# A graph attention layer on one core: messages behind the clip, two products set apart, and 186 instead of 169 column tiles

## The chip, the cores and the metric

The kernel runs on one core of a Trainium2 chip. The metric is device time in microseconds (us), the median of several runs. Engines are named as in the profile: PE (TensorE matmul), PEld (its weight load), DVE (VectorE), ACT (ScalarE), POOL (GpSimd) and SP (SyncE). "DVEq", "ACTq" and so on are the instruction sequencers of these engines, which read the engine's instructions in program order, wait for semaphores and load registers. L12 is line 12 of the kernel.

## What is computed

There are 6,250 nodes with 128 features and 206,250 directed edges, sorted by destination. Each edge has 128 features of its own. The layer is attention with eight heads of 16 features:

```python
Qh, Kh, Vh = (h @ WQ), (h @ WK), (h @ WV)          # per node, 8 heads x 16
Eh = edge_attr @ WE                                # per edge
score = einsum('ehd,ehd,ehd->eh', Kh[src], Qh[dst], Eh) / 4
score = exp(clip(score, -5, 5))
msg = Vh[src] * score[:, :, None]
wV = segment_sum(msg, dst); Z = segment_sum(score, dst)
x = layernorm(x + wV / (Z + 1e-6))
```

## The kernel before

**Tiles, batches, rounds.** The edges are cut into 1612 tiles of 128. Four tiles make a batch (smaller ones at the very end), 406 batches in all. The main loop has one round for each batch b, and different batches stand in it at different stages. From round 12 on the order of the instructions on each engine is the order in which the program writes them.

**Work of a round.** `stage_a(b)` is PE's: for each tile the Q rows of the destinations, by a product with a one-hot matrix (qps, L489), and the projected edge features (eps, L494). `stage_b(b-1)` is DVE's, in four steps between which the loop places other work: kq = K times Q (L500), kqe = kq times E (L503), the sum over each head (sc, L506), and the clip (L509). `weigh(b-1)` is ACT's: the exponential, written twice, into the PSUM tile exp_p (L515) and into the last columns of msg (L517). There is one buffer of exp_p. `messages(b-2)` is DVE's product of V and exp_p (msg, L548). `stage_c(b-2)` is PE's: it adds messages up by destination, with a one-hot matrix (agg, L570); ACT copies such sums to SBUF every fourth batch (L580). `stage_0` and `stage_0t` build the one-hot matrices on DVE for two batches at a time: onehot (L461) in even rounds, between kq and kqe, and onehotT (L477) in odd rounds, between kqe and the head sums.

**Fill steps.** `fill()` issues one small step of what is due beside the main work, if anything is: five DVE steps that split the Q rows of a block of 128 nodes (`q_rows`, L293 to L300), or a step of the normalisation of two blocks (`layernorm`, 22 DVE steps for two blocks, L773 to L793), which begins when ACT has copied its sums (fin, L541). A round has four such places.

**K and V of the sources.** They come into the tile kvrows in two ways. For most tiles POOL gathers 128 rows from a table in HBM (`gather`, L421; one indirect DMA a tile). For 169 tiles, every 11 batches five times, no rows are gathered: the 128 columns of x that belong to the sources are copied one by one out of the transposed x in SBUF (xz) into a tile xcol, PE projects them (`project_columns`, colkv, L403), and ACT places the result in kvrows (`place_columns`, L410). `column_tiles` chooses these tiles from COL0 and COLP.

**Columns.** `columns(b, v, most)` copies runs of COLN = 8 columns: for v = 0 on ACT, eight copies (L394), for v = 1 on DVE, four operations of two columns each (L390). Of the 16 runs of a tile the last six (COLV) are DVE's and ten ACT's. A column's address is read from a register. `addresses` issues the load of eight registers for a run (TENSOR_LOAD, L369), always one run ahead:

```python
at = ahead[v] or addresses(v)   # loaded with the run before
copied[v] += 1
ahead[v] = addresses(v)         # the load for the next run
...                             # then the copies of this run
```

So on each of the two engines the load for the next run stands directly ahead of the copies of this run. The count due grows evenly with b; DVE's 6 runs in 2.2 rounds are mostly three in a round, and the loop gives them three places, one run at each.

**DVE's order in a round** is: kq (b-1); onehot in even rounds; fill; kqe; onehotT in odd rounds; a run; fill; head sums; a run; messages (b-2); the rest of the runs due (one); fill; clip; fill. **ACT's** is: the copy of fin, if due; exp twice; placing; its runs of copies; the copy of agg, if due.

**Pace of the gathers.** The first gather of a batch waits for PE's qps of an earlier batch (`lag`: 12 batches before at first, falling to 3 by about batch 160).

Of the kernel before, what the change touches and what calls it, by code (L numbers as in the profile page):

```python
# [8 lines left out]
F32 = mybir.dt.float32  # L9
I32 = mybir.dt.int32  # L10
BF16 = mybir.dt.bfloat16
U8 = mybir.dt.uint8  # L12
# [4 lines left out]
P = 128  # L17
# [5 lines left out]
HW = 64  # L23
HALF = 16
DRIFT = 24
LEFT, RIGHT = 43, 128
XC = LEFT + N + RIGHT
MW = D + H
CH = 8
# [21 lines left out]
QLOOK = 3  # L51
QREG = 16
COL0 = 26
COLP = (11, 5)
COLN = 8
COLV = 6
COLL = 8
RING = 4096
SUMS = 8
XT_AT = RING + P  # L60
# [3 lines left out]
def cut_batches():  # L64
    out, t = [], 0
    while t < NT:
        k = B
        if t >= NT - TAIL:
            k = 2 if NT - t > 3 else 1
        out.append(range(t, t + k))  # L70
        t += k
    return out


def column_tiles():

    batches = cut_batches()
    at = (COL0 + k * COLP[0] // COLP[1] for k in range(len(batches)))
    return [batches[b][-1] for b in at if b < len(batches) and batches[b][-1] < NT - TAIL - 4 * B]
# [23 lines left out]
def edge_attention(ctx: ExitStack, tc: tile.TileContext, x, xT, srcT, srcC, dstT, dstB, dst0, bnd, lo, eaT,  # L103
                   wq, wkv, we, out, kv, qtab, qs, relD):
    nc = tc.nc
# [25 lines left out]
    nbat = len(batches)  # L131
    col_batches = [t // B for t in column_tiles()]
    col_half = (len(col_batches) + 1) // 2
    col_at = cp.tile([col_half, 2, P], I32, name="col_at")
# [4 lines left out]
    with ExitStack() as fast:  # L139
# [84 lines left out]
        def late_loads():  # L224
            if NT > C0:
                nc.sync.dma_start(src_sb[1], srcT[:, C0:])
                nc.sync.dma_start(dst_sb[:, C0:], dstT[:, C0:])
# [14 lines left out]
        wp = fast.enter_context(tc.tile_pool(name="work", bufs=3))  # L242
# [61 lines left out]
        def build_q(until, now):  # L304

            while qwork or (now and len(built) < until):
                if not qwork:
                    qwork.append(q_rows(len(built)))
                if next(qwork[0], None) is None:
                    qwork.pop()  # L310
                if not now:
                    break
# [23 lines left out]
        def load_chunk(c):  # L336
            if c in chunks or c * CH >= NT:
                return
            n = min(CH, NT - c * CH) * P
            tl = ep.tile([P, CH * P], F32, name="ea")  # L340
            nc.sync.dma_start(tl[:, :n], eaT[:, c * CH * P:c * CH * P + n])
            chunks[c] = tl
# [11 lines left out]
        col_tiles, xz_bytes = {}, xz.rearrange("p n z -> p (n z)").bitcast(U8)  # L354
# [1 line left out]

        copied, projected = [0, 0], []

        runs = P // COLN
        kinds = [range(runs - COLV), range(runs - COLV, runs)]  # L360
        ahead = [None, None]

        def addresses(v):

            k, j = divmod(copied[v], len(kinds[v]))
            if k >= len(col_batches):
                return None
            j = kinds[v][j] * COLN
            return nc.values_load_multi_w_load_instructions(  # L369
                col_at[k % col_half:k % col_half + 1, k // col_half, j:j + COLN],  # L370
                engines=((mybir.EngineType.Activation, mybir.EngineType.DVE)[v],),
                min_val=XT_AT + 8 * LEFT - 4, max_val=XT_AT + 8 * (LEFT + N - 1),
                skip_runtime_bounds_check_because="edges name nodes")[1]

        def columns(b, v, most=runs):

            mine = kinds[v]
            due = int((b - COL0 + COLL) * len(mine) * COLP[1] / COLP[0] + 1e-6)
            while most and copied[v] < min(due, len(col_batches) * len(mine)):
                k, j = divmod(copied[v], len(mine))  # L380
                at = ahead[v] or addresses(v)
                copied[v] += 1
                ahead[v] = addresses(v)
                most -= 1
                if k not in col_tiles:
                    col_tiles[k] = wp.tile([P, P], F32, name="xcol", bufs=5)
                to, j = col_tiles[k].bitcast(U8), mine[j] * COLN
                if v:
                    for c in range(0, COLN, 2):
                        nc.vector.tensor_tensor(to[:, 4 * (j + c):4 * (j + c) + 8], xz_bytes[:, ds(at[c] - XT_AT, 8)],  # L390
                                                xz_bytes[:, ds(at[c + 1] - XT_AT, 8)], op=ALU.bitwise_or)
                else:
                    for c in range(COLN):
                        nc.scalar.copy(to[:, 4 * (j + c):4 * (j + c) + 4], xz_bytes[:, ds(at[c] - XT_AT, 4)])  # L394

        def project_columns(b):

# [8 lines left out]
        def place_columns():  # L406

            while projected:
                g, pk = projected.pop()
                nc.scalar.copy(g[:, B - 1, :], pk)  # L410
# [135 lines left out]
        def messages(b):  # L546
            n, g, m = st8[b]
            nc.vector.tensor_tensor(  # L548
                m[:, :n, :D].rearrange("p b (h d) -> p b h d", h=H),
                g[:, :n, D:].rearrange("p b (h d) -> p b h d", h=H),  # L550
                exp_p[:, :n, :, None].to_broadcast([P, n, H, DH]), op=ALU.mult)
# [47 lines left out]
        build_q(q_built(QLOOK + 2), True)  # L599
        nc.sync.dma_start(col_at, srcC.rearrange("(h p) e -> p h e", h=2))  # L600
        nc.vector.tensor_scalar(col_at, col_at, 8, XT_AT + 8 * LEFT, op0=ALU.mult, op1=ALU.add)
        odd = col_at[:, :, (runs - COLV) * COLN:].rearrange("k h (c z) -> k h c z", z=2)[:, :, :, 1]
        nc.vector.tensor_scalar(odd, odd, 4, None, op0=ALU.subtract)
        load_rel(0)
        for j in range(QLOOK):
# [2 lines left out]
        def fill():  # L608

            if qwork:  # L610
                build_q(0, False)
            elif norms and next(norms[0], None) is None:
                norms.pop(0)

        held = []
        for b in range(nbat + 3):
            if b >= XB and not manual:
                manual.append(fast.enter_context(tc.manual_schedule()))
            held += [(b + SLAG, store) for store in stores]
            stores.clear()  # L620
            if held and (held[0][0] <= b or b >= nbat):
                held.pop(0)[1]()
            if b < nbat:
                load_chunk(batches[b][0] // CH + EB - 3)
                load_rel(batches[b][0] // RC + 1)
                load_q(batches[b][0] // WT + QLOOK)
                g = gathered.pop(b)
                if b == min(XB, nbat - 1):
                    late_loads()
                if b == min(XB + 8, nbat - 1):  # L630
                    relative(C0, NT)
                if b == 14:
                    from_window(1)
                if b == 0:
                    stage_0t(0)
                stage_a(b, g)
                if b + GLEAD < nbat and b + GLEAD not in gathered:
                    gathered[b + GLEAD] = gather(b + GLEAD)
            norms.extend(pending)
            pending.clear()  # L640
            for _ in range(len(ready) if b >= nbat - 2 else 1):
                if ready:
                    finish(ready.pop(0))
            steps = stage_b(b - 1) if 0 <= b - 1 < nbat else iter(())
            next(steps, None)
            if b < nbat:
                stage_0(b)
            fill()
            next(steps, None)
            if b + 1 < nbat:  # L650
                stage_0t(b + 1)
            if b < nbat:
                columns(b, 1, 1)
            fill()
            next(steps, None)
            if b < nbat:
                columns(b, 1, 1)
            if 0 <= b - 2 < nbat:
                messages(b - 2)
            if b < nbat:  # L660
                columns(b, 1)
            fill()
            next(steps, None)
            fill()
            if 0 <= b - 1 < nbat:
                weigh(b - 1)
            place_columns()
            if b < nbat:
                columns(b, 0)
            if 0 <= b - 2 < nbat:  # L670
                stage_c(b - 2)
            if b < nbat:
                project_columns(b + GLEAD)
                build_q(q_built(min(NJ - 1, batches[b][0] // WT + QLOOK + 2)), True)
                if not qwork and len(built) < q_built(
                        min(NJ - 1, batches[min(nbat - 1, b + 3)][0] // WT + QLOOK + 2)):
                    qwork.append(q_rows(len(built)))
                    next(qwork[0])
            if b == min(60, nbat):
                count_inside()  # L680
            if b == min(80, nbat + 1):
                inside = nc.values_load(cnt_i[0:1, 0:1], min_val=0, max_val=2 * EPAD,
                                        skip_runtime_bounds_check_because="two counts of EPAD edges")
# [159 lines left out]
```

## Time and profile before

| | us |
|---|---|
| median of 3 runs | 1866.14 (1864.48 to 1867.87) |
| the profiled execution: its time | 1863.48 |
| the profiled execution: its span | 1861.6 |
| busy: DVE | 1710.0 (92%) |
| busy: ACT | 1576.9 (85%) |
| busy: POOL | 1379.2 (74%) |
| busy: PE, weight loads | 1324.9 (71%), 1156.1 (62%) |
| granted clock of TensorE, mean | 0.927 |

The span is the time between the first and the last instruction on the profiled core. The page gives, for each group of instructions of one line and form, the count, the busy time, the mean duration in ns of one, and behind the second bar the time for which the engine had stood idle just before one of them, with what ended most of it ("issue": nothing that the profile shows). Durations on DVE overlap: an operation that doesn't need the result of the one before starts before that one has ended, so that the distance from start to start, read in the timeline, is what it costs. A register load is executed by the sequencer and does not count as busy.

### The profile page before, as it was taken

To read this page: it belongs to the slowest core of one execution; us is meant where nothing else is said; L and a number is where in the kernel's file an instruction comes from. 1 tells how busy PE (TensorE), PEld (TensorE's weight loads), DVE (VectorE), ACT (ScalarE), POOL (GpSimd) and SP (SyncE) were. 2 spreads that over 40 slices of the span, in tenths; PEclk is the share of its full clock that TensorE was granted. 3 is DMA by queue.
4 is the path that set the end of the run, shared out by engine and by line. 5 is a ranking of instruction groups with operands and counts; after the bars stand their busy time and mean duration, and the time that the engine had idled before them with its cause. 6 is when DMAs were issued, how large, how long until landed. Compare 5 with 4: busy or idle time off the path is not lost.

```text
span 1861.6 us, 49514 instructions
## 1 busy us (share of the span) xinstructions
PE 1324.9 (71%) x9388; PEld 1156.1 (62%) x9388; DVE 1710.0 (92%) x7312; ACT 1576.9 (85%) x14716; POOL 1379.2 (74%) x1450
## 2 busy tenths in 40 slices
PE   5877777677677767777767776776767676777775
PEld 4766666566566666666656665665656665666665
DVE  6579999999999999999999999999999999999986
ACT  3327999899999999999999999999989998999950
POOL 7777777767777777677777777777777777777774
PEclk8888998899999999899998899899999999999997
DMA  9767677667766776677677667767766676677652
GB/s 303 228 214 217 184 217 206 197 187 207 212 199 183 212 214 184 209 214 208 183 225 210 190 188 225 206 184 211 224 202 185 202 223 190 196 200 233 205 173 68
DMA packets 170093, 377.79 MB, mean 203 GB/s; under 512 B 58305, under 2 KB 84245, under 8 KB 169775
## 3 DMA queue, kind: packets, MB, share of 16 engines
q0 software_dynamic: 68480, 186.02, 34.7%
q1 hardware_dynamic: 100155, 187.47, 33.6%
q14 instruction: 241, 1.97, 0.3%
q8 instruction: 77, 1.26, 0.3%
q10 hardware_dynamic: 1140, 1.06, 0.2%
HBM read 359.61 MB, written 14.81 MB: 201 GB/s over the span
## 4 chain that ended last, share of the span: by engine, by line
DVE 38%; DMA 17%; ACT 16%; PE 9%; POOL 7%; issue 6%; DVEq 5%; ACTq 2%; SPq 0%; POOLq 0%
DMA kvrows<-kv,src 14%; ACT xcol L394 13%; DVE xcol L390 7%; POOL kvrows L421 7%; DVE kqe L503 6%; DVE kq L500 6%; DVE sc L506 6%; DVE msg L548 5%; DVEq L369 5%; PE agg L570 3%; DVE onehotT L477 2%; PE eps L494 2%; ACTq L369 2%; PE finps L529 1%; DVE sc L509 1%
## 5 line engine op out<-in xcount | busy, mean ns | idle before, releaser
L421 POOL DMA_INDIRECT kvrows<-kv,src x1395 | 1329.7, 953 | 445.1 <-issue 307.7
L394 ACT COPY xcol<-xz 128x4 uint8 x13520 | 1364.8, 190 | 55.0 <-issue 49.4
L570 PE MATMUL agg<-msg,onehot 128*128 128x136 f32 x3224 | 511.6, 305 | 283.7 <-DVE msg L548 216.6
L570 PEld LDWEIGHTS agg<-msg,onehot 128*128 128x128 f32 x3224 | 442.0, 206 | 335.9 <-issue 302.6
L494 PE MATMUL eps<-we_sb,ea 128*128 128x128 f32 x3224 | 494.3, 299 | 149.3 <-DVE kqe L503 110.8
L494 PEld LDWEIGHTS eps<-we_sb,ea 128*128 128x128 f32 x3224 | 423.7, 205 | 200.2 <-DVE kqe L503 149.8
L390 DVE TENSOR_TENSOR xcol<-xz 128x8 uint8 x4056 | 399.5, 157 | 2.8 <-issue 1.7
L500 DVE TENSOR_TENSOR kq<-kvrows,qps 128x512 f32<-128x512 f32 x406 | 273.4, 673 | 38.3 <-DMA kvrows<-kv,src 29.0
L503 DVE TENSOR_TENSOR kqe<-kq,eps 128x512 f32<-128x512 f32 x406 | 274.5, 676 | 19.7 <-PE eps L494 4.7
L548 DVE TENSOR_TENSOR msg<-kvrows,exp_p 128x512 f32<-128x512 f32 x406 | 272.9, 672 | 4.6 <-ACT exp_p L515 4.6
L506 DVE TENSOR_REDUCE sc<-kqe 128x32 f32<-128x512 f32 x406 | 271.0, 667 | 0.5
L489 PE MATMUL qps<-qw,onehotT 126*128 126x128 bf16 x1612 | 168.6, 230 | 39.0 <-DVE kq L500 32.6
L489 PEld LDWEIGHTS <-onehotT 126*128 126x128 bf16 x1612 | 134.3, 103 | 84.9 <-issue 58.4
L515 ACT ACTIVATE exp_p<-sc 128x32 f32<-128x32 f32 x406 | 79.3, 195 | 92.1 <-DVE sc L509 79.3
L461 DVE TENSOR_TENSOR onehot<-iota_p,dst_sb 128x512 f32<-128x512 f32 x200 | 135.9, 680 | 3.0 <-PE agg L570 3.0
L529 PE MATMUL finps<-sum,shift 128*128 128x136 f32 x640 | 94.8, 292 | 30.0 <-ACT sum L580 29.8
L403 PE MATMUL colkv<-wkv_sb,xcol 128*128 128x256 f32 x338 | 114.5, 424 | 0.0
L477 DVE TENSOR_SCALAR onehotT<-relb,node 126x1024 bf16<-126x1024 bf16 (+2 forms) x206 | 103.7, 504 | 9.7 <-DMA relb<-relD 9.7
L529 PEld LDWEIGHTS finps<-sum,shift 128*128 128x128 f32 x640 | 83.3, 197 | 37.4 <-ACT sum L580 37.3
L517 ACT ACTIVATE msg<-sc 128x32 f32<-128x32 f32 x406 | 87.1, 215 | 0.1
L509 DVE TENSOR_SCALAR sc<-sc 128x32 f32<-128x32 f32 x406 | 77.0, 190 | 0.3
L421 POOL DMA_INDIRECT kvrows<-x,src x48 | 48.6, 1012 | 16.5 <-issue 12.2
(76 smaller groups left out, 567.2 us busy)
## 6 DMA issues: line engine op xcount, KB each, us to landing
ea<-eaT SPq DMA_DIRECT2D x201, 512.0 KB
relb<-relD SPq DMA_DIRECT2D x100, 504.0 KB
kvrows<-kv,src POOLq DMA_INDIRECT x1395
qw<-qs SPq DMA_DIRECT2D x202, 31.5 KB
kv<-ea SPq DMA_DIRECT2D x12, 512.0 KB
qs<-qst SPq DMA_DIRECT2D x48, 96.0 KB
xb<-x SPq DMA_DIRECT2D x24, 128.0 KB
out<-h SPq DMA_DIRECT2D x24, 128.0 KB
```

Source lines behind the costliest of these rows:

```text
L390: nc.vector.tensor_tensor(to[:, 4 * (j + c):4 * (j + c) + 8], xz_bytes[:, ds(at[c] - XT_AT, 8)], xz_bytes[:, ds(at[c + 1] - XT_AT, 8)], op ...
L394: nc.scalar.copy(to[:, 4 * (j + c):4 * (j + c) + 4], xz_bytes[:, ds(at[c] - XT_AT, 4)])
L421: ins = nc.gpsimd.indirect_dma_start(out=g[:k, i, :f], out_offset=None, in_=rows, in_offset=bass.IndirectOffsetOnAxis(ap=src_col(t)[:k], a ...
L477: nc.vector.tensor_scalar(ohT[:, :w], rels[t0 // RC][:, e0:e0 + w], node[:QROWS], None, op0=ALU.is_equal)
L489: expanded[b] = nc.tensor.matmul(pq[:, i, :], ohT[:, i * P:i * P + P], loaded[t0 // WT], start=True, stop=True)
L494: nc.tensor.matmul(pe[:, i, :], ea[:, i * P:i * P + P], we_sb, start=True, stop=True)
L500: nc.vector.tensor_tensor(t0[:, :n], g[:, :n, :D], pq[:, :n], op=ALU.mult)
L503: nc.vector.tensor_tensor(t1[:, :n], t0[:, :n], pe[:, :n], op=ALU.mult)
L506: nc.vector.tensor_reduce(sc[:, :n], t1[:, :n].rearrange("p b (h d) -> p b h d", h=H), axis=AX.X, op=ALU.add)
L529: nc.tensor.matmul(ps, shift[:, P - s:2 * P - s], sums[k // 2][:, k % 2], start=first and i == 0, stop=stop and i == len(parts) - 1)
L548: nc.vector.tensor_tensor(m[:, :n, :D].rearrange("p b (h d) -> p b h d", h=H), g[:, :n, D:].rearrange("p b (h d) -> p b h d", h=H), exp_p[ ...
L570: nc.tensor.matmul(aggs[u][:, 0 if final else k % 2], oh[:, i, :], m[:, i, :], start=not final and t % (2 * G) == 0, stop=tail)
```

## The change

The diff does these things:

- COLP goes from (11, 5) to (2, 1): a column tile every two batches, 186 instead of 169. DVE's six runs a tile are then three in every round, and ACT's ten are five.
- The cut into runs is written in a new way (COL2 = 8, COLV = 48 columns); the runs are the same as before, eight columns each, ten of ACT's and six of DVE's.
- The order on DVE becomes: kq (b-1); in even rounds onehot, in odd rounds a fill and one run; kqe; in odd rounds onehotT, in even rounds one run; two fills; head sums; the rest of the runs due (two); fill; clip; messages (b-2). The next round's kq follows.
- The transposed x loses its margins (LEFT 43 and RIGHT 128 become 1 and 1), and xcol has six buffers instead of five.

```diff
-LEFT, RIGHT = 43, 128
+LEFT, RIGHT = 1, 1
...
-COLP = (11, 5)
+COLP = (2, 1)
 COLN = 8
-COLV = 6
+COL2 = 8
+COLV = 48
...
-                    col_tiles[k] = wp.tile([P, P], F32, name="xcol", bufs=5)
+                    col_tiles[k] = wp.tile([P, P], F32, name="xcol", bufs=6)
...
             if b < nbat:
                 stage_0(b)
-            fill()
+            if b % 2:
+                fill()
+            if b < nbat and b % 2:
+                columns(b, 1, 1)
             next(steps, None)
             if b + 1 < nbat:
                 stage_0t(b + 1)
-            if b < nbat:
+            if b < nbat and b % 2 == 0:
                 columns(b, 1, 1)
             fill()
+            fill()
             next(steps, None)
-            if b < nbat:
-                columns(b, 1, 1)
-            if 0 <= b - 2 < nbat:
-                messages(b - 2)
             if b < nbat:
                 columns(b, 1)
             fill()
             next(steps, None)
-            fill()
+            if 0 <= b - 2 < nbat:
+                messages(b - 2)
             if 0 <= b - 1 < nbat:
                 weigh(b - 1)
             place_columns()
```

`next(steps, None)` issues, in this order, kq (ahead of the lines shown), kqe, the head sums and the clip.

More of the change, by code (lines that the diff above doesn't have):

```diff
@@ L357, in edge_attention @@
         copied, projected = [0, 0], []
-        runs = P // COLN
-        kinds = [range(runs - COLV), range(runs - COLV, runs)]
+        mid = P - COLV
+        few, pairs2 = -(-mid // COLN), COLV // COL2
+        cut = [mid * i // few for i in range(few + 1)] + [mid + COL2 * (i + 1) for i in range(pairs2)]
+        pieces = list(zip(cut, cut[1:]))
+        kinds = [pieces[:few], pieces[few:]]
         ahead = [None, None]
@@ L367, in addresses @@
                 return None
-            j = kinds[v][j] * COLN
+            i, j = kinds[v][j]
             return nc.values_load_multi_w_load_instructions(
-                col_at[k % col_half:k % col_half + 1, k // col_half, j:j + COLN],
+                col_at[k % col_half:k % col_half + 1, k // col_half, i:j],
                 engines=((mybir.EngineType.Activation, mybir.EngineType.DVE)[v],),
@@ L373, in addresses, with columns @@
                 skip_runtime_bounds_check_because="edges name nodes")[1]
-        def columns(b, v, most=runs):
+        def columns(b, v, most=P):
             mine = kinds[v]
@@ L385, in columns @@
                 if k not in col_tiles:
-                    col_tiles[k] = wp.tile([P, P], F32, name="xcol", bufs=5)
-                to, j = col_tiles[k].bitcast(U8), mine[j] * COLN
+                    col_tiles[k] = wp.tile([P, P], F32, name="xcol", bufs=6)
+                to, (i, e) = col_tiles[k].bitcast(U8), mine[j]
                 if v:
-                    for c in range(0, COLN, 2):
-                        nc.vector.tensor_tensor(to[:, 4 * (j + c):4 * (j + c) + 8], xz_bytes[:, ds(at[c] - XT_AT, 8)],
+                    for c in range(0, e - i, 2):
+                        nc.vector.tensor_tensor(to[:, 4 * (i + c):4 * (i + c) + 8], xz_bytes[:, ds(at[c] - XT_AT, 8)],
                                                 xz_bytes[:, ds(at[c + 1] - XT_AT, 8)], op=ALU.bitwise_or)
                 else:
-                    for c in range(COLN):
-                        nc.scalar.copy(to[:, 4 * (j + c):4 * (j + c) + 4], xz_bytes[:, ds(at[c] - XT_AT, 4)])
+                    for c in range(e - i):
+                        nc.scalar.copy(to[:, 4 * (i + c):4 * (i + c) + 4], xz_bytes[:, ds(at[c] - XT_AT, 4)])
         def project_columns(b):
@@ L601, in edge_attention @@
         nc.vector.tensor_scalar(col_at, col_at, 8, XT_AT + 8 * LEFT, op0=ALU.mult, op1=ALU.add)
-        odd = col_at[:, :, (runs - COLV) * COLN:].rearrange("k h (c z) -> k h c z", z=2)[:, :, :, 1]
+        odd = col_at[:, :, mid:].rearrange("k h (c z) -> k h c z", z=2)[:, :, :, 1]
         nc.vector.tensor_scalar(odd, odd, 4, None, op0=ALU.subtract)
```

## The prediction

> **What bounds the kernel now.** I read the page's busy shares and its chain of waits first, then the busy time by stretch, then the instructions of single rounds on VectorE (DVE), in order of time.
>
> ```profile
> PE 1324.9 (71%) x9388; PEld 1156.1 (62%) x9388; DVE 1710.0 (92%) x7312; ACT 1576.9 (85%) x14716; POOL 1379.2 (74%) x1450
> DVE 38%; DMA 17%; ACT 16%; PE 9%; POOL 7%; issue 6%; DVEq 5%; ACTq 2%; SPq 0%; POOLq 0%
> ```
>
> ```profile
> 600.00:700.00 100.00, 69.09 (x513) 60.47 (x514) 97.06 (x444) 94.14 (x898) 73.52 (x78) 0.97 0.69 206
> 1200.00:1300.00 100.00, 69.66 (x522) 60.76 (x522) 95.38 (x425) 92.94 (x878) 75.76 (x80) 0.97 0.68 195
> 146.00:1790.00 1644.00, 1168.49 (x8452) 1023.13 (x8452) 1564.01 (x6966) 1522.24 (x14526) 1230.61 (x1292) 0.94 0.70 203
> ```
>
> The columns of the second block are the stretch, its length, and busy time with count for PE, PE's weight loads, DVE, ACT and POOL, then clock, DMA share and GB/s. Three engines lie close together. Early DVE leads (97%). From about 900 us on POOL is full as well: 80 gathers in 100 us are 1.25 us each, and each gather, though it is busy for 0.95, is followed by 0.30 in which POOL takes nothing. So fewer gathers help only if DVE and ACT can follow. The third row is the stage that the change touches, from the first copied column to the last: 1644 us. Here is what DVE did there when it was not busy, 80 us in all, by group:
>
> ```profile
> L503 DVE TENSOR_TENSOR kqe<-kq,eps 128x512 f32<-128x512 f32 x371 | 252.2, 680 | 13.6 <-DVE kq L500 0.9 <-DVE v L784 0.4 <-PE qps L489 0.2
> L500 DVE TENSOR_TENSOR kq<-kvrows,qps 128x512 f32<-128x512 f32 x371 | 251.1, 677 | 22.5 <-DMA kvrows<-kv,src 17.9 <-issue 1.5 <-ACT msg L517 0.8
> L297 DVE CAST qst<-qrows 128x128 bf16<-128x128 f32 (+1 forms) x43 | 12.4, 288 | 16.2 <-PE qrows L293 16.2
> L773 DVE TENSOR_SCALAR rz<-fin 128x16 f32<-128x16 f32 x23 | 4.9, 213 | 25.0 <-ACT fin L541 24.8
> ```
>
> 371 rounds in 1644 us are 4.43 us each. Only 17.9 us of DVE's idle time is for gathered rows, so late gathers cost the kernel little: **DVE's own queue is the bound**, with POOL and ACT just behind it. One even round and the start of an odd one, on DVE:
>
> ```profile
> 1012.06 0.69 DVE L500 TENSOR_TENSOR kq<-kvrows,qps 128x512 f32<-128x512 f32 x1 [0.71 <-issue]
> 1012.66 0.68 DVE L461 TENSOR_TENSOR onehot<-iota_p,dst_sb 128x512 f32<-128x512 f32 x1
> 1013.26 0.68 DVE L503 TENSOR_TENSOR kqe<-kq,eps 128x512 f32<-128x512 f32 x1
> 1013.86 0.44 DVE L390 TENSOR_TENSOR xcol<-xz 128x8 uint8 x4
> 1014.22 0.67 DVE L506 TENSOR_REDUCE sc<-kqe 128x32 f32<-128x512 f32 x1
> 1014.81 0.38 DVE L390 TENSOR_TENSOR xcol<-xz 128x8 uint8 x4
> 1015.12 0.68 DVE L548 TENSOR_TENSOR msg<-kvrows,exp_p 128x512 f32<-128x512 f32 x1
> 1015.71 0.38 DVE L390 TENSOR_TENSOR xcol<-xz 128x8 uint8 x4
> 1016.02 0.20 DVE L509 TENSOR_SCALAR sc<-sc 128x32 f32<-128x32 f32 x1
> 1016.11 0.67 DVE L500 TENSOR_TENSOR kq<-kvrows,qps 128x512 f32<-128x512 f32 x1
> 1016.88 0.69 DVE L503 TENSOR_TENSOR kqe<-kq,eps 128x512 f32<-128x512 f32 x1
> 1017.49 0.48 DVE L477 TENSOR_SCALAR onehotT<-relb,node 126x1024 bf16<-126x1024 bf16 x1
> 1017.89 0.39 DVE L390 TENSOR_TENSOR xcol<-xz 128x8 uint8 x4
> ```
>
> Read start to start: a large operation takes 0.60, a run of four xcol 0.31 (1014.81 to 1015.12), onehotT 0.40, the clip 0.09. With onehot behind it kq takes 0.60; with the dependent kqe right behind, 0.77.
>
> **The register loads.** Each run of eight columns is preceded in program order by a load of eight addresses (L369), for the run after it. It isn't counted as busy, so the timeline omits it. These are its rows: all loads of DVE; two inside the even round above; the longest one.
>
> ```profile
> L369 DVEq TENSOR_LOAD <-col_at x1014: 591/607/1211, 144.2 to 1787.7; - x169
> L369 DVEq TENSOR_LOAD <-col_at x2: 594/596/598, 1014.0 to 1014.8; - x2
> L369 DVEq TENSOR_LOAD <-col_at x1: 1211/1211/1211, 710.4 to 710.4; - x1
> ```
>
> What DVE did behind the longest one, and, from the chain in order of time, the first load of the even round:
>
> ```profile
> 710.91 0.48 DVE L477 TENSOR_SCALAR onehotT<-relb,node 126x1024 bf16<-126x1024 bf16 x1
> 711.67 0.41 DVE L390 TENSOR_TENSOR xcol<-xz 128x8 uint8 x4 [0.28 <-issue]
> ```
>
> ```profile
> 1012.87 0.60 DVEq L369
> ```
>
> The load issued at 710.4 returned at 711.61, and the next run began at 711.67 behind 0.28 of idle time, although its own addresses had come with the load before. So **what stands behind a load in program order waits for it**; only what was queued ahead of it covers it. And a load waits for what stands ahead of it. The first load of the even round went out at 1012.87. It returned at 1013.47, and four xcol and the reduce were free to be queued then; yet the second went out only at 1014.0, when kqe had ended (1013.26 + 0.68 = 1013.94). The reduce needs kqe, and its wait held up the load behind it. The third followed 0.8 later.
>
> **The change part by part.** The sum is made against the profiled execution, 1863.5 us with a span of 1861.6; the median of the runs shown, 1866.1, is 0.15% above it.
>
> *More tiles.* 17 more tiles bring 17 x 6 = 102 runs to DVE: 102 x 0.31 = **+31 us**. Three runs stand in every round now, not 2.7.
>
> *Other work between the products.* In the odd rounds a run, and a step of the normalisation if one is due, stands between kq and kqe: 186 x (0.77 - 0.60) = **-32 us**. (The even rounds had onehot there already.) [...]
>
> *Two runs in a row.* Before, the three runs of a round stand apart, with a large operation between any two. After, one stands early and two directly behind the reduce, with one load between them and nothing else. Count from the start T of kqe. The load ahead of the second run goes out when kqe has ended, T + 0.73. The next load is 0.82 behind it (0.60, and some 0.22 to hand over four xcol; the row above has 0.8 with one more instruction), so T + 1.55; it returns after 0.60, and the third run begins some 0.08 later: T + 2.23. In an even round DVE has work until T + 0.60 + 0.31 (run) + 0.60 (reduce) + 0.31 (run) = T + 1.82 and then stands idle for 0.41. In an odd round onehotT (0.40) takes the place of the first run: T + 1.91, 0.32 idle. Over 186 rounds of each, 186 x 0.73 = **+136 us**. The trace of before has no two such runs in a row, so I bound it: nothing if the second load is covered after all (an idle stretch can't be negative), and 372 x (0.60 + 0.08) = 253 us if the whole of a load is bare each time. I take the count, since each of its pieces has its own row. Behind the bare load stand the third run, the clip and the messages; for the messages wait ACT's exp (exp_p is a single buffer which they read) and PE's sums.
>
> *Two fill steps side by side.* These are the small steps of the normalisation and of the Q rows, mostly dependent on each other: 23 x 22 + 43 x 5 = 721 in this stage by the counts above, spread over 3.5 places a round, so about 206 pairs. At most each pays what kq paid ahead of kqe, 0.17: 35 us; at least nothing. I take +25, nearer that row, as most steps of a pair depend on one another.
>
> *Gathers.* 17 fewer are 21 us less of POOL, which is no longer the bound: seven gathers in two rounds are 8.75 us, against the 9.6 that DVE needs below. DVE's wait for gathered rows goes, **-18 us**. The waits for fin and qrows (41 us) I leave as they are; if they went, that much would come off.
>
> *At nothing.* The clip ahead of the messages: the second and third runs cover its wait for the reduce, and the exp behind it can't start sooner, since the messages must have read exp_p first. ACT's 1360 more copies and PE's 17 more projections lie beside DVE's longer round; without that cover ACT would be the bound (below). The narrower xT and the sixth xcol buffer: under 1 us in the head, and the waits name no xcol buffer.
>
> Sum: 31 - 32 + 136 + 25 - 18 = +142, so 1863.5 + 142 = **2005 us**, or 4.81 us a round.
>
> **Rivals.**
>
> ```profile
> L394 ACT COPY xcol<-xz 128x4 uint8 x13520 | 1364.8, 190 | 55.0 <-issue 49.4
> ```
>
> ```profile
> L369 ACTq TENSOR_LOAD <-col_at x1690: 537/557/1039, 148.0 to 1792.1; - x188
> ```
>
> ```profile
> 200.00:800.00 600.00, 426.48 (x3125) 373.67 (x3124) 577.24 (x2566) 559.23 (x5363) 439.55 (x462) 0.95 0.70 204
> ```
>
> ```profile
> L515 ACT ACTIVATE exp_p<-sc 128x32 f32<-128x32 f32 x137 | 26.6, 194 | 12.1 <-DVE sc L509 10.1 <-DVE mv L782 1.6
> L541 ACT COPY fin<-finps 128x136 f32<-128x136 f32 x17 | 4.6, 273 | 12.3 <-PE finps L529 12.3
> ```
>
> 1. *The loads are covered, and ACT is the bound.* DVE would then need 1644 + 31 - 32 + 25 - 18 = 1650 us, as now. The last three rows are of 200 to 800 us: ACT's round there is 600 / 137 = 4.38, without its waits for exp_p and fin (24.4 / 137) 4.20. A run of copies costs it 1364.8 / 1690 = 0.81, and it gets 5 runs a round instead of 4.55, with a little more placing: 4.20 + 0.37 + 0.02 = 4.59. Over 372 rounds that is 1707, +63: **1926 us**. For it: the first load of a round is covered now. Against it: the idle time behind the load of 710.4. [...]
>
> 2. *Faster: POOL's 17 gathers are what counts.* If DVE's loads are covered and ACT keeps each round within 3.5 gathers, 4.375 us, the gain is 17 x 1.25 = 21: **1842 us**. It decides only if ACT's 40 copies and the rest stay under 4.375, and ACT's waits above leave it 4.59. For it: POOL's 80 gathers in 100 us.
>
> 3. *ACT falls in with the messages.* Its exp now waits for the last large operation of DVE's round. If its queue stands at that wait every time, its next load (0.56) is bare as well: exp 0.25, load 0.6, five runs 4.05, placing and sums 0.2, about 5.1 a round, 372 x 5.1 - 1644 = +253: **2117 us**. Against it: ACT's exp may come almost a round late before the next messages need it.
>
> **How the numbers follow.** Forecast 0.70, rival 1 0.15, rival 2 0.06, rival 3 0.07, and 0.02 that slack on all sides swallows it. About 0.2% is what a measurement of this kernel can tell from no change; so faster 0.06, same 0.02, slower 0.92. The forecast's own range is 1950 (fin and qrows waits gone, fill pairs free) to 2050 (half as much again bare of each load). Reaching to rival 1, and leaving out rivals 2 and 3, the range is 1920 to 2055.
>
> **What would show it.** On DVE, an idle "issue" stretch of 0.3 to 0.4 between the two runs behind the reduce, in nearly every round, as idle time ahead of L390 of over 100 us (2.8 us on the page of before); no stall between kq and kqe; DVE's wait for gathered rows near zero; fewer gathers in 100 us than 80 (7 in 9.6 us are 73); ACT waiting longer at exp_p. If L390 shows no such idle time, the step on two runs in a row is wrong, and rival 1 or 2 decides. If ACT is busy without a wait at exp_p, rival 1 or 3 holds.

## The result, and the profile after

The changed kernel takes 2011.4 us (median of 4 runs, 2010.4 to 2013.5), against 1865.8: a ratio of 1.078, 95% interval 1.076 to 1.080. The forecast was 2005, with a range of 1920 to 2055. Four runs below (the first ones of experiments 1 and 2, and experiments 3 and 4) come from a slower chip, on which the kernel before took 2543 us and ACT stood idle in them for 470 to 528 us between its column copies, for a cause that stays open, so their times and ratios are not set beside the others, for which the kernel before took 1862 to 1866 us.

The first page lines of the changed kernel are its busy times and its chain of waits:

```profile
PE 1402.2 (70%) x9422; PEld 1238.3 (62%) x9422; DVE 1767.0 (88%) x7720; ACT 1718.6 (86%) x16093; POOL 1367.0 (68%) x1433
DVE 35%; ACT 26%; issue 9%; DMA 8%; DVEq 7%; PE 6%; POOL 5%; ACTq 3%; POOLq 0%; SPq 0%
```

DVE does 57 us more work, but its share fell from 92% to 88%: it stands idle more. Its groups say where. The number to read is the one behind the bar that follows the mean duration, the idle time ahead of the group. First three groups of the kernel before, then four of the changed one:

```profile
L390 DVE TENSOR_TENSOR xcol<-xz 128x8 uint8 x4056 | 399.5, 157 | 2.8 <-issue 1.7
L503 DVE TENSOR_TENSOR kqe<-kq,eps 128x512 f32<-128x512 f32 x406 | 274.5, 676 | 19.7 <-PE eps L494 4.7 <-DVE kq L500 0.9 <-PE qps L489 0.7
L773 DVE TENSOR_SCALAR rz<-fin 128x16 f32<-128x16 f32 x24 | 5.1, 212 | 26.7 <-ACT fin L541 26.6
```

```profile
L394 DVE TENSOR_TENSOR xcol<-xz 128x8 uint8 x4464 | 445.6, 159 | 141.1 <-issue 139.3
L504 DVE TENSOR_TENSOR kq<-kvrows,qps 128x512 f32<-128x512 f32 x406 | 273.3, 673 | 12.6 <-DMA kvrows<-x,src 4.7 <-ACT kvrows L448 3.4 <-issue 2.5
L507 DVE TENSOR_TENSOR kqe<-kq,eps 128x512 f32<-128x512 f32 x406 | 272.5, 671 | 4.3 <-PE eps L498 3.2
L778 DVE TENSOR_SCALAR rz<-fin 128x16 f32<-128x16 f32 x24 | 5.0, 206 | 26.5 <-ACT fin L545 26.4
```

Ahead of the column copies stood 2.8 us of idle time; now it is 141.1, and its releaser is "issue", so no other engine and no transfer ended it, as far as the profile shows. DVE's wait at kq for rows gathered from the table (17.9 us in the column stage before) is down to 1.7. The wait for ACT's fin is as it was.

Added up by place in the round, 125 of the 141 us stand ahead of the third run, in 356 of 372 rounds. Another 13.5 stand ahead of the first run of the odd rounds, which the change moved between kq and kqe.

One odd round of the changed kernel, on DVE in order of time, with the loads of that stretch from the view of line 373 (formerly 369) in a fence of their own:

```profile
999.94 0.67 DVE L507 TENSOR_TENSOR kqe<-kq,eps 128x512 f32<-128x512 f32 x1
1000.54 0.48 DVE L481 TENSOR_SCALAR onehotT<-relb,node 126x1024 bf16<-126x1024 bf16 x1
1000.94 0.67 DVE L510 TENSOR_REDUCE sc<-kqe 128x32 f32<-128x512 f32 x1
1001.53 0.38 DVE L394 TENSOR_TENSOR xcol<-xz 128x8 uint8 x4
1002.22 0.42 DVE L394 TENSOR_TENSOR xcol<-xz 128x8 uint8 x4 [0.30 <-issue]
1002.57 0.17 DVE L513 TENSOR_SCALAR sc<-sc 128x32 f32<-128x32 f32 x1
1002.65 0.68 DVE L552 TENSOR_TENSOR msg<-kvrows,exp_p 128x512 f32<-128x512 f32 x1
1003.25 0.68 DVE L504 TENSOR_TENSOR kq<-kvrows,qps 128x512 f32<-128x512 f32 x1
```

```profile
L373 DVEq TENSOR_LOAD <-col_at x2: 614/618/621, 1000.7 to 1001.5; - x2
```

This is the count of the prediction, piece by piece. kqe ends at 1000.61, the load ahead of the second run goes out at 1000.7, the next one 0.8 later at 1001.5; it takes 0.61 and returns at about 1002.13; the third run starts at 1002.22. From the second run's start to the third's are 0.69 where the work of a run is 0.31: 0.38 are lost. (The idle column says 0.30, since the last copy of the second run was still finishing.) Over the rounds of the stage that loss has a median of 0.44 in even rounds without fill steps and 0.36 in odd ones; the prediction had 0.41 and 0.32.

The third run did not wait for its own addresses: they had come with the load that went out at 1000.7 and was back at 1001.29. What it waited for is the return of the load for the run after it. In the whole changed kernel none of the 1115 runs on DVE that stand behind a load began before that load had returned; the closest began 0.09 us behind it. On ACT it is the same with 1859 runs, the closest 0.07 us behind.

The 13.5 us ahead of the odd rounds' first run are bare loads too, of a kind that the prediction did not count. Here is one of them, with the load of that stretch:

```profile
237.98 0.24 DVE L778 TENSOR_SCALAR rz<-fin 128x16 f32<-128x16 f32 x1 [0.47 <-ACT fin L545]
238.69 0.40 DVE L394 TENSOR_TENSOR xcol<-xz 128x8 uint8 x4 [0.46 <-issue]
```

```profile
L373 DVEq TENSOR_LOAD <-col_at x1: 601/601/601, 238.0 to 238.0; - x1
```

rz, the first step of a normalisation, waits for ACT's fin and holds up the load behind it; when it goes, DVE has nothing else queued, and the run starts only when the load is back. That happens in 23 rounds, for a median of 0.53, 13.0 us in all.

Busy time in two stretches, columns as in the prediction:

```profile
900.00:1700.00 800.00, 552.95 (x3780) 490.38 (x3781) 719.66 (x3285) 742.67 (x7094) 552.99 (x581) 0.88 0.62 187
146.00:1935.00 1789.00, 1245.30 (x8453) 1105.31 (x8452) 1611.02 (x7325) 1657.09 (x15838) 1218.35 (x1274) 0.88 0.61 185
```

581 gathers in 800 us are 73 in 100 us (forecast 73, before 80 there): POOL is no longer full. The stage with column copies takes about 1789 us for some 371 rounds, 4.82 each (forecast 4.81).

### The profile page after: what moved, and what is told of

Read it like the earlier page. It is cut to its first block, busy times and chain, and to the rows that moved or that the text cites. A ratio compares the mean times of both kernels' runs of the same rounds, so it can differ in the third digit from the quotient of the medians.

```text
span 2008.5 us, 51313 instructions
## 1 busy us (share of the span) xinstructions
PE 1402.2 (70%) x9422; PEld 1238.3 (62%) x9422; DVE 1767.0 (88%) x7720; ACT 1718.6 (86%) x16093; POOL 1367.0 (68%) x1433
## 4 chain that ended last, share of the span: by engine, by line
DVE 35%; ACT 26%; issue 9%; DMA 8%; DVEq 7%; PE 6%; POOL 5%; ACTq 3%; POOLq 0%; SPq 0%
ACT xcol L398 23%; DVE xcol L394 8%; DVEq L373 7%; DMA kvrows<-kv,src 6%; DVE kq L504 5%; DVE kqe L507 5%; POOL kvrows L425 5%; DVE msg L552 5%; DVE sc L510 3%; ACTq L373 3%; DVE onehotT L481 2%; PE agg L574 2%; DVE sc L513 1%; PE finps L533 1%; PE kvps L447 1%
## 5 line engine op out<-in xcount | busy, mean ns | idle before, releaser
L398 ACT COPY xcol<-xz 128x4 uint8 x14880 | 1498.2, 191 | 55.1 <-issue 44.7
L574 PE MATMUL agg<-msg,onehot 128*128 128x136 f32 x3224 | 546.0, 319 | 456.7 <-DVE msg L552 433.6
L574 PEld LDWEIGHTS agg<-msg,onehot 128*128 128x128 f32 x3224 | 470.4, 217 | 514.6 <-issue 324.9
L394 DVE TENSOR_TENSOR xcol<-xz 128x8 uint8 x4464 | 445.6, 159 | 141.1 <-issue 139.3
L498 PE MATMUL eps<-we_sb,ea 128*128 128x128 f32 x3224 | 526.8, 313 | 58.1 <-DVE kqe L507 54.3
L498 PEld LDWEIGHTS eps<-we_sb,ea 128*128 128x128 f32 x3224 | 459.1, 219 | 93.8 <-DVE kqe L507 88.7
L493 PE MATMUL qps<-qw,onehotT 126*128 126x128 bf16 x1612 | 182.3, 243 | 11.8 <-DVE kq L504 9.9
L493 PEld LDWEIGHTS <-onehotT 126*128 126x128 bf16 x1612 | 145.7, 111 | 60.0 <-issue 29.4
L519 ACT ACTIVATE exp_p<-sc 128x32 f32<-128x32 f32 x406 | 79.8, 196 | 101.7 <-DVE msg L552 95.7
L407 PE MATMUL colkv<-wkv_sb,xcol 128*128 128x256 f32 x372 | 138.6, 461 | 0.0
L407 PEld LDWEIGHTS colkv<-wkv_sb,xcol 128*128 128x128 f32 x372 | 70.9, 233 | 0.0
```

The source lines that it names most:

```text
L394: nc.vector.tensor_tensor(to[:, 4 * (i + c):4 * (i + c) + 8], xz_bytes[:, ds(at[c] - XT_AT, 8)], xz_bytes[:, ds(at[c + 1] - XT_AT, 8)], op ...
L398: nc.scalar.copy(to[:, 4 * (i + c):4 * (i + c) + 4], xz_bytes[:, ds(at[c] - XT_AT, 4)])
L407: nc.tensor.matmul(pk, col_tiles.pop(k), wkv_sb, start=True, stop=True)
L493: expanded[b] = nc.tensor.matmul(pq[:, i, :], ohT[:, i * P:i * P + P], loaded[t0 // WT], start=True, stop=True)
L498: nc.tensor.matmul(pe[:, i, :], ea[:, i * P:i * P + P], we_sb, start=True, stop=True)
L574: nc.tensor.matmul(aggs[u][:, 0 if final else k % 2], oh[:, i, :], m[:, i, :], start=not final and t % (2 * G) == 0, stop=tail)
```

## The experiments

The theory (A) is that two runs in a row leave a register load bare on DVE, and that this sets the time. The main rival is that the 17 more tiles, with 1360 more copies on ACT, set it.

**1. The third run behind the messages.** This takes the two runs apart and leaves the clip ahead of the messages and the 186 tiles.

```diff
             if b < nbat:
-                columns(b, 1)
+                columns(b, 1, 1)
             fill()
             next(steps, None)
             if 0 <= b - 2 < nbat:
                 messages(b - 2)
+            if b < nbat:
+                columns(b, 1)
```

> The changed kernel with one edit: the third run of a round stands behind the messages instead of directly behind the second run, so that the messages (0.60 us) lie over its load. Clip ahead of messages, 186 tiles, five ACT runs a round all stay. Theory A (a bare register load on DVE between two runs in a row): idle time ahead of the column copies on DVE falls from 141 us to under 15, and 2011 - 136 = 1875 us if DVE alone sets the time; if ACT is the next bound, up to the 1926 us worked out for it. Rival (186 tiles are too many copies for ACT, and DVE's idle time is only slack): the time stays above 1990 us.

> The third run behind the messages once more, since on the chip of the first four experiments all kernels took a third longer, with ACT standing idle between its copies (491 us of 'issue'), which the profiles of before and after don't show. Same expectation as for the first time. Theory A: idle time ahead of DVE's column copies under 15 us (it was 28.9 on that chip, 141 in the changed kernel), and a ratio to the kernel before of 1.005 to 1.035 instead of 1.078, depending on where ACT's own bound lies. Rival (ACT's copies): ratio above 1.065.

The first time, on the slower chip: 2618 us, ratio 1.029 (1.024 to 1.035). The second time: **1934.5 us**, ratio 1.039 (1.037 to 1.040). On DVE then:

```profile
L394 DVE TENSOR_TENSOR xcol<-xz 128x8 uint8 x4464 | 444.9, 158 | 20.2 <-issue 15.4
L780 DVE TENSOR_SCALAR rz<-fin 128x16 f32<-128x16 f32 x24 | 4.8, 201 | 77.0 <-ACT fin L545 76.9
```

Ahead of the third run only 2.3 us of idle time are left, and 77 us of the time went with the rest. (Of the 20.2 that remain ahead of all column copies, forecast under 15, 15.0 stand ahead of the odd rounds' first run.) So two runs in a row cost at least that, and the rival's "above 1.065" is out. But 73 us of the slowdown stay, and the ratio is just over the range given. DVE now waits 77 us for fin, an output of ACT (26.5 before the edit). Another bound has come up behind the first, close to the 1926 us which rival 1 of the prediction worked out for ACT.

**2. 169 tiles in the new order.** The edit is `COLP = (11, 5)` in the changed kernel.

> The changed kernel with the old number of column tiles (169, every 11 batches five); the new order stays. Theory A: two runs stand in a row in the 73% of rounds that have three runs, so 0.73 x 372 x 0.365 = 99 us of bare loads are left: 1863.5 - 32 + 99 + 25 - 18 = 1938 us, between 1920 and 1955. Rival (ACT's copies): ACT has its old number of runs back, so about 1866 us, at most 1885.

> The changed kernel with 169 tiles, once more on a chip that runs as in the profiles of before and after. Theory A (bare loads between two runs in a row on DVE): two runs stand in a row in 73% of the rounds; 99 us of idle time ahead of the column copies, 1938 us, between 1915 and 1955. Rival (17 more tiles are what costs): about 1866 us.

On the slower chip 2555 us, ratio 1.004 (1.001 to 1.007). Then **1930.4 us**, ratio 1.035 (1.034 to 1.037), against 1938 by theory A and 1866 by the rival. The idle time is there without a single additional tile; 90 of the 105 us stand ahead of the third run, against the 99 counted:

```profile
L394 DVE TENSOR_TENSOR xcol<-xz 128x8 uint8 x4056 | 406.0, 160 | 105.3 <-issue 103.5
```

**3. 186 tiles in the old order.** The edit is `COLP = (2, 1)` in the kernel before.

> The kernel before with 186 column tiles and nothing else changed: three runs in every round, each behind a large operation. Theory A: no bare loads. DVE alone would give 1863.5 + 31 - 18 = 1877 us, ACT by its own price 1926; so between 1870 and 1930, and DVE idle ahead of its column copies under 10 us. Rival (the 17 tiles themselves cost the time): about 2000 us.

Only tried on the slower chip: 2603 us, ratio 1.024 (1.018 to 1.029). The idle time ahead of the column copies is 10.3 us, just over the 10 expected, as theory A needs in an order without two runs in a row. The time says little on that chip.

**4. Runs of sixteen on DVE.** The edit is `COL2 = 16` in the changed kernel.

> The changed kernel with DVE's columns cut into runs of sixteen instead of eight: three runs in two rounds, never two in a row, one load of sixteen registers for each. Theory A: if such a load takes about what one of eight takes, the idle time ahead of the column copies falls under 20 us and the time to 1875 to 1930 us; if it takes twice as long (1.2 us), some 0.1 to 0.4 us stays in the rounds that have a second run, so 1890 to 1970 us. Rival (ACT): ACT's copies are as many as before, so above 1990 us.

Also on the slower chip only: 2615 us, ratio 1.027 (1.022 to 1.032), no verdict on the time. The load itself is the result:

```profile
L373 DVEq TENSOR_LOAD <-col_at x558: 1093/1124/1339, 198.5 to 2529.2; - x186
```

Sixteen registers take 1.12 us where eight take 0.61 (medians). Half as many loads, each nearly twice as long: 149.5 us of idle time ahead of the column copies remained, and the hope for under 20 fell. Only 56 of them stand ahead of the second run of a round; 93 stand ahead of the first, where the expectation had put none.

**5. Other work between the products, alone.** The kernel before, with its first run between kq and kqe in odd rounds.

```diff
             fill()
+            if b < nbat and b % 2:
+                columns(b, 1, 1)
             next(steps, None)
             if b + 1 < nbat:
                 stage_0t(b + 1)
-            if b < nbat:
+            if b < nbat and b % 2 == 0:
                 columns(b, 1, 1)
```

> The kernel before with one part of the change alone: in odd rounds the first run of DVE's columns stands between kq and kqe instead of behind onehotT; 169 tiles, all else as before. By the step on other work between the products: the distance from kq to kqe goes from 0.77 to 0.60 in odd rounds, 32 us of DVE in all; in the second half, where POOL is full, DVE then waits for gathers instead, so 1840 to 1860 us. [...]

1870.0 us, ratio 1.004 (1.002 to 1.006): no gain, rather a trace of a loss, and my expectation fell. The profile shows that the edit did its work and that the saving went elsewhere:

```profile
L390 DVE TENSOR_TENSOR xcol<-xz 128x8 uint8 x4056 | 400.6, 157 | 20.5 <-issue 16.8
L503 DVE TENSOR_TENSOR kqe<-kq,eps 128x512 f32<-128x512 f32 x406 | 272.9, 672 | 6.4 <-PE eps L494 4.8 <-PE qps L489 0.5
L775 DVE TENSOR_SCALAR rz<-fin 128x16 f32<-128x16 f32 x24 | 4.7, 197 | 33.7 <-ACT fin L541 33.5
```

The idle time ahead of kqe fell from 19.7 to 6.4 us; that ahead of the column copies rose from 2.8 to 20.5, and that for ACT's fin from 26.7 to 33.7. Of the 20.5, 18.9 stand ahead of the moved run itself, 13.2 of them in 23 rounds where rz stands directly ahead of its load, as shown above for the changed kernel. So the edit brought bare loads of its own, which the expectation had not counted, and its null does not show by itself that something other than DVE bounds the kernel before. Nor does it say that a run between the two products saves nothing: in the changed kernel, whose odd rounds have the same order there, a run starts at 1009.19, 0.60 after a kq of 0.67, and kqe 0.31 behind the run:

```profile
1008.59 0.67 DVE L504 TENSOR_TENSOR kq<-kvrows,qps 128x512 f32<-128x512 f32 x1
1009.19 0.38 DVE L394 TENSOR_TENSOR xcol<-xz 128x8 uint8 x4
1009.50 0.67 DVE L507 TENSOR_TENSOR kqe<-kq,eps 128x512 f32<-128x512 f32 x1
```

**6. ACT made light**, in the changed kernel and in that of experiment 1. Each run of ACT copies eight adjacent columns from the first address instead of eight from their own, so it leaves out the other seven of each run, and only the time counts.

```diff
-                    for c in range(e - i):
-                        nc.scalar.copy(to[:, 4 * (i + c):4 * (i + c) + 4], xz_bytes[:, ds(at[c] - XT_AT, 4)])
+                    nc.scalar.copy(to[:, 4 * i:4 * e], xz_bytes[:, ds(at[0] - XT_AT, 4 * (e - i))])
```

> The changed kernel with ACT made light: each run of eight column copies on ACT is one copy of the same bytes in number (so the columns that ACT delivers are wrong ones, and the margin on the right is 8). ACT's loads, its exp and all of DVE's work stay. Theory A: DVE's queue alone sets the time of the changed kernel, so 2011 us hardly moves: 1985 to 2012, the gain at most DVE's wait for ACT's fin (26 us). Rival (ACT's copies set it): under 1900 us.

> The third run behind the messages and ACT made light in the same way (columns from ACT are wrong ones). That took 1934.5 us with ACT's copies. If what was left there is ACT's own bound, as rival 1 of the prediction priced it (1926), it falls to what DVE alone or POOL's gathers need: 1845 to 1885 us. If DVE still bounds it, it stays within 10 us of 1934.

In the changed kernel: **1979.1 us**, ratio 1.060 (1.058 to 1.062), 6 us below the range of theory A and far from the rival's. With an ACT that has next to nothing to copy, 114 of the 146 us remain, and so does the idle time:

```profile
L394 DVE TENSOR_TENSOR xcol<-xz 128x8 uint8 x4464 | 448.6, 161 | 133.8 <-issue 131.3
L777 DVE TENSOR_SCALAR rz<-fin 128x16 f32<-128x16 f32 x24 | 5.2, 218 | 6.8 <-ACT fin L544 6.8
```

Of the 32 us that went, 20 are DVE's wait for fin (26.5 to 6.8). With the runs apart: **1847.2 us**, ratio 0.990 (0.989 to 0.992), 87 us less than with ACT's copies. So what was left in experiment 1 was ACT. What bounds then is POOL, full at 80 gathers in 100 us, as in the kernel before, and DVE, busy for 97%:

```profile
900.00:1700.00 800.00, 583.19 (x4160) 512.81 (x4159) 779.64 (x3610) 300.70 (x1433) 606.36 (x636) 0.92 0.70 205
```

This kernel is 18 us faster than the kernel before, near the 21 that rival 2 gave for the 17 gathers spared. But ACT was made light in it as well, and no run tells the two apart; with ACT's copies in place the same tiles are a loss.

**7. The first run back behind onehotT**, in odd rounds of the changed kernel.

```diff
             if b % 2:
                 fill()
-            if b < nbat and b % 2:
-                columns(b, 1, 1)
             next(steps, None)
             if b + 1 < nbat:
                 stage_0t(b + 1)
-            if b < nbat and b % 2 == 0:
+            if b < nbat:
                 columns(b, 1, 1)
```

> The changed kernel with one edit: in odd rounds the first run goes back from between kq and kqe to behind onehotT. Counted as in the prediction, two things happen in each of 186 odd rounds: kq to kqe costs 0.77 instead of 0.60 (+32 us in all), and DVE has a run (0.31 us) more to do while the two loads behind kqe are under way, so that 0.31 of idle time goes (-58 us). Theory A: 26 us faster than the changed kernel, 1975 to 1995 us, and idle time ahead of the column copies of 75 to 95 us. Rival (the run between the products saves its 32 us whatever else): 2030 to 2045 us.

2007.0 us, ratio 1.076 (1.075 to 1.078): between the two. My count had left out a load. Moved back, the first run's own load comes behind kqe too, so three loads at some 0.83 from start to start lie between kqe and the third run, where I had counted two. With that, the odd rounds without fill steps lose 0.24 (median) instead of 0.36, not zero. The idle time ahead of the column copies fell by 20 us, to 120.7 (half of it ahead of the third run, half ahead of the first, which no longer has a load behind rz), and the dependent kqe took nearly all of that back.

**8. The order alone: runs apart and 169 tiles.** Experiment 1's edit and `COLP = (11, 5)` in the changed kernel.

> The changed kernel with the third run behind the messages and 169 tiles: what is left of the change is the order alone (other work between the products, clip ahead of the messages, two fills side by side). It is the fourth corner beside 2011 (two runs in a row, 186 tiles), 1930 (in a row, 169) and 1934 us (apart, 186). If DVE's bare loads and ACT's copies are the only two costs and each hides part of the other, it comes out at 1855 to 1875 us, level with the kernel before. If the new order costs something of its own, it is above 1880.

**1866.7 us**, ratio 1.0012 (1.0003 to 1.0021): level to 2 us. This is the fourth corner:

| median, us | 169 tiles | 186 tiles |
|---|---|---|
| third run behind the messages | 1866.7 | 1934.5 |
| second and third run in a row | 1930.4 | 2011.4 |

Two runs in a row cost 64 and 77 us; 17 tiles cost 68 and 81. Clip ahead of messages, work between the products and fills side by side come to nothing together there.

**9. The fills apart.** In the changed kernel the second of the two fills moves behind the clip.

```diff
             fill()
-            fill()
             next(steps, None)
             if b < nbat:
                 columns(b, 1)
             fill()
             next(steps, None)
+            fill()
```

> The changed kernel with the second of the two fills side by side moved behind the clip, ahead of the messages. By the prediction's step a pair costs DVE up to 0.17 us, 206 pairs, taken as 25 us, and the idle stretch behind the reduce is the same or shorter by a fill: 1976 to 1995 us. If pairs are free (the second step hides behind what is queued): 2005 to 2015 us.

1975.3 us, ratio 1.059 (1.058 to 1.061): 36 us less, slightly past the expected end. 196 pairs became 11. But only part of the 36 is what the prediction's step priced, one step waiting for another: DVE's busy time fell by 15 us. The idle time ahead of the column copies fell by 21, since behind a pair the loads come later (in the changed kernel the load ahead of the second run goes out 0.46 us behind the end of kqe in even rounds with a pair and 0.53 in odd ones, 0.05 in rounds without fill steps; medians): in rounds with fill steps the loss between the two runs fell from medians of 0.46 and 0.38 to 0.33 and 0.28.

None of these beats the kernel before, apart from the one with the runs apart that leaves out most of ACT's columns (experiment 6).

## Why the prediction held, step by step

- *Two runs in a row, +136 us.* Right, and shown: 125 us of idle time stand ahead of the third run, where the prediction put them, with the loads at the times counted, and they go when the row is taken apart (experiment 1). Taken from start to start the loss is larger, about 0.43 on average in 372 rounds, 158 us; some 19 of it come from the fill pairs (experiment 9), and the pieces of 0.41 and 0.32 were a little short.
- *More tiles, +31 us.* DVE's copies are busy 46 us longer (399.5 to 445.6), of which 408 more of them at a mean step of 0.08 make 32.
- *Work between the products, -32 us.* Too large. The idle time ahead of kqe went (19.7 to 4.3 us), but beside experiment 7, where the run is back, the distance from kq to kqe is shorter by 0.18 only in the 96 odd rounds without a fill step there, and by 0.07 in 67 with one (the run's own 0.31 taken off): about 22 us. And 13 are lost again behind rz, which the step did not count.
- *Fills side by side, +25 us.* The count was near: 196 pairs, for the 206 foretold (the Q rows of a block are four fill steps of DVE, not five; with four it is 678 steps and 194 pairs). The price was too high: taking the pairs apart is worth 36, but 21 of these are longer bare loads, and some 15 are left for the pairs themselves.
- *Gathers, -18 us.* Right: DVE's wait for gathered rows is down to 1.7 us, and POOL does 73 gathers in 100 us.
- *ACT's 1360 copies at nothing, under cover of DVE.* Nearly: with all of ACT's copies made light the changed kernel gains 32 us, 20 of them DVE's wait for fin and 7 the bare loads behind rz, so ACT adds that much through what DVE waits for. The price without the cover, 1926 us, was measured as 1934.5.
- *"DVE's own queue is the bound"* of the kernel before was put too sharply. The kernel of experiment 8 is level with it, and against that one the light kernel of experiment 6 with the runs apart keeps DVE busy for 33 us more, in the same order (1745.6 against 1712.3), and is still 20 us faster. So in these kernels DVE also waits out what ACT and POOL need. This didn't hurt, since the change made DVE the slowest.
- ACT "waiting longer at exp_p" was a weak sign: idle time ahead of L519 is 101.7 us, against 92.1 before.
- The sum came out at +142, and 146 were measured. That it is so close is partly luck: with the sizes that the runs show, the same five terms give 32 - 9 + 158 + 15 - 27 = +169 (27 is the fall of the wait for gathered rows in the whole kernel, 29.0 to 1.7). So other waits shrank, or the terms overlap, by some 23 us; the wait for qrows fell from 16.2 to 6.9, the rest no run tells. The two ends of the forecast's own range don't follow from the reasons given for them: 2005 less 41 and 25 is 1939, not 1950, and 2005 plus half of 136 is 2073, not 2050.

## What to carry to other kernels

A register load in an engine's instruction stream was no background work in these kernels: on DVE and ACT no run of copies in the changed kernel began before the load ahead of it had returned (the closest 0.09 and 0.07 us behind it). So a load of eight registers needed 0.61 us of queued work ahead of it here, and two of them with a run of 0.31 between them could not both have that. A load right behind an instruction that waits for another engine was bare as well (0.53 us in 23 rounds here). Count the loads between a dependent operation and the instruction that needs them, each at its full start-to-start distance (0.8 us here), before moving work around. And where three engines are near full, as here, look at all three: with the runs apart, 17 tiles cost 68 us, more than the 31 us of work that they bring to DVE, and what they cost went with ACT's copies.

## What was not expected

- A load's length went almost with its registers: on DVE 0.61 us for eight, 1.12 for sixteen (medians, experiment 4).
- The granted clock of TensorE went down with the bare loads: 0.927 before and 0.923 with the runs apart, 0.892 and 0.878 with two in a row (169 and 186 tiles), 0.875 with two in a row and ACT light. PE waits more for messages there (its idle time ahead of the agg products is 456.7 us, 283.7 before). Whether the longer pauses bring the clock down was not tried.
